# Seven conditional expert tiles, and all loads of the last stage ahead of its outputs

## The chip, the cores and the metric

The kernel runs on one core of one Trainium2 chip. The metric is the time of one execution on the device in microseconds; of several executions the median counts. One further execution was taken by the hardware profiler; its page and trace are what the rows in this document come from. Engines are written as in the profile: PE is TensorE (PEld its weight loads), DVE is VectorE, ACT is ScalarE, POOL is GpSimd, SP is SyncE, which here only issues transfers. A `q` behind a name (SPq, POOLq) is the engine's sequencer.

## The reference

The program computes two layers on an image of 256 channels and 48 x 48 positions, that is 2304 tokens of 256 numbers, all in float32. The first layer is a group norm and a full softmax attention over 9216 rows. The second is a sliced attention and then a mixture of experts. Only the mixture of experts and the way out matter here:

```python
gate_logits = xf @ Wg + bg                      # 2304 tokens x 8 experts
top_w, top_i = jax.lax.top_k(gate_logits, 2)    # two experts for each token
top_w = jax.nn.softmax(top_w, axis=-1)
...
for e in range(E):
    h = jax.nn.gelu(xf @ W1[e] + b1[e], approximate=False)      # 256 -> 1024
    out = out + w_dense[:, e:e + 1] * (h @ W2[e] + b2[e])       # 1024 -> 256
...
t = t + out            # then the tokens are turned back into the image's layout
```

The reference multiplies every token with every expert and weights all but two of the products with zero. So 2 x 2304 = 4608 (token, expert) pairs do count.

## The kernel before

**Tiles of experts.** The kernel sorts the 4608 pairs by expert, and fills tiles of 128 rows, each tile with pairs of one expert only. An expert's last tile is seldom full. How many tiles are needed depends on the data: at least 36 (4608 / 128), and at most 43, which is `NSL = (2 * NT - E) // P + E`. The kernel before always works off 43 tiles. Those that no pair fills belong, by the clamp of `expert_i` to 7, to the last expert, and their rows point at spare rows behind the tokens. Three tables are computed on the chip before the stage begins: `expert_i` (the expert of each tile), `slot_t` (the token's row for each of the 128 rows of each tile) and `slot_w` (the weight of each row). `ends` holds the running sum of the tiles of experts 0 to 7, so its last entry is the number of tiles in use.

**One tile.** `load(s)` gathers 128 normed tokens from DRAM (`tn_d`) into `xs` with an indirect transfer that POOL issues (L1018), and loads the expert's first weights, 1 MB, into `w1` with a transfer that SP issues (L1025). `turn` transposes `xs` on PE into `pt` and DVE copies it to `xT`. `first(s)` multiplies with `w1` into `ph`, and ACT makes `hid` with gelu. `second(s)` multiplies `hid` with `w2_sb`, which holds the second weights of all experts, into `py`; DVE adds the bias and applies the weight into `y`; and POOL issues an indirect transfer that adds `y` to the tokens in DRAM, `t_d` (L1075). Each engine that needs the number of the tile's expert loads it into a register for itself (`expert_of`, L1004).

**The order of the tiles.** The stage is a software pipeline, written out by hand: in round s, `load(s + 2)` is asked for, then `first(s)` is done, then `second(s - 1)`, and after three of the eight steps of that `second` the transposes of tile s + 1 are put in between (`meanwhile`). PE, DVE, ACT and in places POOL keep this written order (the class `InOrder`; each operation issued through it has line L55 in the profile). The indirect transfers and the weight loads are not held to the written order; the framework's scheduler places them. Buffers come from pools: two each of `xs`, `w1`, `xT`, `hid`, `y`, three banks of `ph`, two of `py` and of `pt`.

**The last stage.** The 2304 tokens are read back from `t_d` in five blocks (`TBLOCKS`: four of 512 tokens and one of 256) into `tt`, turned on PE into `pt` (L1127), copied to `ob` by DVE (L1131) and ACT (L1133), and written out (L1134). Loads (L1120) and outputs are both issued by SP, in the order load, output, block by block as the scheduler finds them ready. The pool `fin` has three buffers of `tt` and of `ob`.

**The one condition that is there already.** The attention is computed without subtracting a maximum; the verdict `bad` says whether that was safe. At the end every engine loads `bad` (L1142) and branches (`tc.If(again > 0)`, L1145): the whole program a second time, with the maximum, or nothing. In the runs shown the second pass is not taken. In the arm that is not taken, every engine brings its semaphores to the counts that they would have after the body. L1177 is the program's end, with its drains and the closing barrier.

Of the kernel before, what the change touches and what calls it, by code (L numbers as in the profile page):

```python
# [1 line left out]

# [6 lines left out]
FP = mybir.dt.float32  # L9
AF = mybir.ActivationFunctionType  # L10
ALU = mybir.AluOpType
AX = mybir.AxisListType
PSUM = bass.MemoryType.PSUM

P = 128
C = 256
NT = 2304
# [12 lines left out]
E = 8  # L30
HID = 1024
NHC = HID // P
BIG = 1.5 * 2.0**30


NSL = (2 * NT - E) // P + E


TBLOCKS = [(t, min(512, NT - t)) for t in range(0, NT, 512)]
# [21 lines left out]
def layers(  # L61
# [11 lines left out]
    nc = tc.nc  # L73
    x_v = x[0].rearrange("(c p) h w -> p c (h w)", p=P)
    out_v = out[0].rearrange("(c p) h w -> p c (h w)", p=P)

    const = ctx.enter_context(tc.tile_pool(name="const", bufs=1))
    pe, dve, act, pool = (InOrder(tc, e) for e in (nc.tensor, nc.vector, nc.scalar, nc.gpsimd))
    small = ctx.enter_context(tc.tile_pool(name="small", bufs=2))


# [8 lines left out]
        out=gmat, in_=gmat, pattern=[[-8, 16], [0, 8]], compare_op=ALU.is_ge,  # L90
# [3 lines left out]
        out=gmat, in_=gmat, pattern=[[8, 16], [0, 8]], compare_op=ALU.is_ge,  # L94
# [14 lines left out]
        out=not_before, in_=not_before, pattern=[[-1, P]], compare_op=ALU.is_ge,  # L109
# [96 lines left out]
    for h in range(H1):  # L206
        at = ((h // 2) % 2 * 2 + h // 4) * D1
        nc.sync.dma_start(
            out=Wout_sb[at : at + D1, h % 2, 0:C], in_=Wout[h * D1 : (h + 1) * D1, :]
# [23 lines left out]
    with proj, tc.tile_pool(name="ps_pj", bufs=5, space=PSUM) as ps_pj, tc.tile_pool(  # L233
        name="ps_w", bufs=2, space=PSUM
# [41 lines left out]
        for bi, (t0, tn) in enumerate(TBLOCKS):  # L276
# [6 lines left out]
            for m in range(2):  # L283
# [11 lines left out]
                for j in range(2):  # L295
                    rows = slice(j * DK, (j + 1) * DK)
                    at = (2 * m + j) * NT + t0
# [397 lines left out]
        nc.sync.dma_start(out=w2_sb[:, e], in_=W2[e].rearrange("(f p) d -> p f d", p=P))  # L695
    b2_bc = wts.tile([P, E * C], FP, name="b2_bc")
    nc.sync.dma_start(out=b2_bc, in_=b2.rearrange("e d -> (e d)").partition_broadcast(P))
    fp = ctx.enter_context(tc.tile_pool(name="ffn", bufs=2))
    route = ctx.enter_context(tc.tile_pool(name="route", bufs=1))
    gating = ExitStack()  # L700
    gp = gating.enter_context(tc.tile_pool(name="gate", bufs=1))
# [2 lines left out]
    with tc.tile_pool(name="sa", bufs=1) as sa:  # L704
        tw = sa.tile([P, C + E], FP, name="tw")
        with sums_done, tc.tile_pool(name="ps_b", bufs=4, space=PSUM) as ps_b, tc.tile_pool(
            name="ps_sc", bufs=1, space=PSUM
        ) as ps_sc:
            dve.tensor_tensor(ts_sum, ts_sum, pts, ALU.add)
            ph = ps_b.tile([P, 2, S], FP, name="ph", tag="mm")  # L710
# [63 lines left out]
            a = sa.tile(by_head, FP, name="a")  # L774
# [89 lines left out]
            normed(NTT - 6)  # L864


    expert_i = route.tile([1, NSL], mybir.dt.int32, name="expert_i")
    slot_w = route.tile([P, NSL], FP, name="slot_w")
    slot_t = route.tile([P, NSL], mybir.dt.int32, name="slot_t")
# [2 lines left out]
    with gating, tc.tile_pool(name="onehot", bufs=1) as oh, tc.tile_pool(  # L872
# [121 lines left out]
        ex = gp.tile([P, NSL], FP, name="ex")  # L994
        dve.tensor_reduce(ex, past, AX.X, ALU.add)
        dve.tensor_scalar(expert_i, ex[0:1, :], float(E - 1), None, ALU.min)
        empties = gp.tile([P, NSL], FP, name="empties")
        dve.tensor_scalar(empties, pw[:, 0, :], 0.0, spare, ALU.is_equal, ALU.mult)
        dve.scalar_tensor_tensor(empties, pw[:, 0, :], -1.0, empties, ALU.add, ALU.add)
# [6 lines left out]
            skip_runtime_bounds_check_because="it is counted from 0 and cut at E - 1",  # L1006
        )

    with tc.tile_pool(name="ps_h", bufs=3, space=PSUM) as ps_h, tc.tile_pool(
        name="ps_y", bufs=2, space=PSUM  # L1010
    ) as ps_y, tc.tile_pool(name="ps_t", bufs=2, space=PSUM) as ps_t, tc.tile_pool(
        name="ps_j", bufs=1, space=PSUM
    ) as ps_j:

        def load(s):

            xs = fp.tile([P, C], FP, name="xs", tag="xs")
            nc.gpsimd.indirect_dma_start(  # L1018
                out=xs, out_offset=None, in_=tn_d[:, :],
                in_offset=bass.IndirectOffsetOnAxis(ap=slot_t[:, s : s + 1], axis=0),  # L1020
                bounds_check=NT + P - 1, oob_is_err=True,
            )
            w1 = fp.tile([P, 2, HID], FP, name="w1", tag="w1")
            e = expert_of(s, mybir.EngineType.SP)
            nc.sync.dma_start(  # L1025
                out=w1, in_=W1[bass.ds(e, 1)].rearrange("e (c p) f -> p (e c) f", p=P)
            )
            return xs, w1

        def turn(xs):  # L1030

            pt = ps_t.tile([P, 2, P], FP, name="pt", tag="pt")
            for c in range(2):
                pe.transpose(pt[:, c, :], xs[:, c * P : (c + 1) * P], ident)
            xT = fp.tile([P, 2, P], FP, name="xT", tag="xT")
            dve.tensor_copy(xT, pt)
            return xT

        def first(s, xT, w1):

            e = expert_of(s, mybir.EngineType.Activation)
            hid = fp.tile([P, NHC, P], FP, name="hid", tag="hid")
            for f0 in range(0, NHC, 4):
                ph = ps_h.tile([P, 4, P], FP, name="ph", tag="ph")
                for f in range(f0, f0 + 4):
                    for c in range(2):
                        pe.matmul(
                            ph[:, f - f0, :], w1[:, c, f * P : (f + 1) * P], xT[:, c, :],
                            start=(c == 0), stop=(c == 1),
                        )  # L1050
                for f in range(f0, f0 + 4):
                    act.activation(
                        hid[:, f, :], ph[:, f - f0, :], AF.Gelu, bias=b1_e[:, bass.ds(e, 1), f],
                    )
            return hid

        def second(s, hid, meanwhile):

            e = expert_of(s, mybir.EngineType.PE)
            py = ps_y.tile([P, C], FP, name="py", tag="py")  # L1060
            for f in range(NHC):
                pe.matmul(
                    py, hid[:, f, :],
                    w2_sb[:, bass.ds(e, 1), f, :].rearrange("p e d -> p (e d)"),
                    start=(f == 0), stop=(f == NHC - 1),
                )
                if f == 2:
                    meanwhile()
            e = expert_of(s, mybir.EngineType.DVE)
            y = fp.tile([P, C], FP, name="y", tag="y")  # L1070
            dve.tensor_tensor(
                y, py, b2_e[:, bass.ds(e, 1), :].rearrange("p e d -> p (e d)"), ALU.add
            )
            dve.tensor_scalar(y, y, slot_w[:, s : s + 1], None, ALU.mult)
            nc.gpsimd.indirect_dma_start(  # L1075
                out=t_d[:, :], out_offset=bass.IndirectOffsetOnAxis(ap=slot_t[:, s : s + 1], axis=0),
                in_=y, in_offset=None, bounds_check=NT + P - 1, oob_is_err=True,
                compute_op=ALU.add,
            )

        loaded = {s: load(s) for s in range(2)}
        turned, hid = {}, {}

        def turn_next(s):
            if s < NSL:
                xs, w1 = loaded.pop(s)
                turned[s] = turn(xs), w1

        def judge():

            both = fp.tile([P, 2], FP, name="both", tag="judge")
            for k, op in enumerate((ALU.max, ALU.min)):
                dve.tensor_reduce(both[:, k : k + 1], ends_of[:, k, :], AX.X, op)
            dve.tensor_scalar(both[:, 0:1], both[:, 0:1], HIGH, None, ALU.is_gt)
            dve.tensor_scalar(both[:, 1:2], both[:, 1:2], LOW, None, ALU.is_lt)
            dve.tensor_tensor(both[:, 0:1], both[:, 0:1], both[:, 1:2], ALU.max)
            pm = ps_j.tile([1, P], FP, name="pm")
            pe.transpose(pm, both[:, 0:1], ident)
            dve.tensor_reduce(bad, pm, AX.X, ALU.max)

        turn_next(0)
        for s in range(NSL):
            if s + 2 < NSL:
                loaded[s + 2] = load(s + 2)
            hid[s] = first(s, *turned.pop(s))
            if s == 0:
                turn_next(1)
            else:
                second(s - 1, hid.pop(s - 1), lambda: turn_next(s + 1))
            if s == 4 and bad is not None:  # L1110
                judge()
        second(NSL - 1, hid.pop(NSL - 1), lambda: None)


    with tc.tile_pool(name="fin", bufs=3) as fin, tc.tile_pool(
        name="ps_f", bufs=4, space=PSUM
    ) as ps_f:
        for t0, n in TBLOCKS:
            tt = fin.tile([P, 4, C], FP, name="tt", tag="tt")
            nc.sync.dma_start(  # L1120
                out=tt[:, 0 : n // P, :], in_=t_d[t0 : t0 + n, :].rearrange("(i p) c -> p i c", p=P)
            )
            ob = fin.tile([P, 2, 512], FP, name="ob", tag="ob")
            for c in range(2):
                pt = ps_f.tile([P, 512], FP, name="pt", tag="pt")
                for k in range(n // P):
                    nc.tensor.transpose(  # L1127
                        pt[:, k * P : (k + 1) * P], tt[:, k, c * P : (c + 1) * P], ident
                    )
                if c == 0:  # L1130
                    nc.vector.tensor_copy(ob[:, c, 0:n], pt[:, 0:n])  # L1131
                else:
                    nc.scalar.copy(ob[:, c, 0:n], pt[:, 0:n])  # L1133
            nc.sync.dma_start(out=out_v[:, :, t0 : t0 + n], in_=ob[:, :, 0:n])  # L1134


@with_exitstack
# [44 lines left out]
```

## Time and profile before

| | us |
|---|---|
| median of three executions | 1675.54 (1674.44 to 1675.96) |
| the profiled execution, its own time | 1674.74 |
| its span in the profile | 1672.9 |
| PE busy in the span | 1603.6 (96%) |
| first `xs` gather of the expert stage starts at | 1324.44 |
| last matmul `py` of the expert stage ends at | 1643.23 |
| first load of the last stage starts at | 1649.23 |

Times in rows of the timeline are microseconds from the start of the span: start, duration, engine, line, operation, output and inputs by the program's names, and, in brackets, how long the engine had been idle and what ended that. Rows of the page's slices cut the span into 40 equal parts of 41.8 us; a digit is the busy share in tenths, and PEclk is the clock that TensorE was granted. Durations of matmuls are modelled at their end and overlap a little with the next.

### The profile page before, as it was taken

What the parts mean: (1) busy time and instruction counts of PE and PEld (TensorE: products, weight loads), DVE (VectorE), ACT (ScalarE), POOL (GpSimd) and SP (SyncE); (2) the same over time, 40 slices, a digit from 0 to 9 for tenths busy, and PEclk for the clock granted to TensorE, in tenths of its full rate; (3) what the DMA queues carried; (4) which work ended last, traced back from release to release, by engine and by line L of the source; (5) the groups of instructions that cost most, each with busy time, mean ns of one, the idle gap of its engine ahead of it and who ended that gap; (6) DMA issues with size and microseconds to landing.
All of it is one profiled execution on the core that took longest, in us unless ns stands there. A gap on an engine that the chain in (4) does not pass through costs nothing.

```text
span 1672.9 us, 32258 instructions
## 1 busy us (share of the span) xinstructions
PE 1603.6 (96%) x13376; PEld 821.5 (49%) x13376; DVE 1051.3 (63%) x1371; ACT 819.3 (49%) x1132; POOL 156.5 (9%) x133
## 2 busy tenths in 40 slices
PE   7999999999999999999999999999987699999994
PEld 3633343333333333333333333333334699999994
DVE  6577777778687787787787886877865511111111
ACT  2355565565565555555655655655532133322331
POOL 0000000000000000000000000000001333333331
PEclk9999999999999999999999999999996599999997
DMA  4000000000000000000000000000007366666664
GB/s 132 1 1 1 1 1 1 1 1 1 2 1 1 1 1 2 1 1 1 1 1 1 1 1 1 1 1 1 2 30 269 116 198 174 179 185 189 179 168 125
DMA packets 41267, 82.91 MB, mean 50 GB/s; under 512 B 3693, under 2 KB 26810, under 8 KB 40986
## 3 DMA queue, kind: packets, MB, share of 16 engines
q1 hardware_dynamic: 32858, 69.49, 12.4%
q0 software_dynamic: 8256, 11.28, 3.9%
q8 instruction: 108, 1.77, 0.4%
q14 instruction: 45, 0.37, 0.1%
HBM read 67.78 MB, written 12.98 MB: 48 GB/s over the span
## 4 chain that ended last, share of the span: by engine, by line
PE 77%; issue 11%; POOL 6%; DVE 3%; DMA 2%; ACT 0%; POOLq 0%; SPq 0%; ACTq 0%; DVEq 0%
PE s L55 33%; PE av L55 33%; POOL t_d L1075 3%; POOL xs L1018 2%; PE pa L55 2%; PE ph L55 2%; PE pb L55 1%; DMA t_d<-y,slot_t 1%; PE pw L55 1%; PE py L55 1%; PE pp L288 1%; PE pp L292 1%; PE pp L317 1%; DMA tt<-t_d 0%; DVE s L55 0%
## 5 line engine op out<-in xcount | busy, mean ns | idle before, releaser
L55 DVE TENSOR_TENSOR acc<-acc,p 128x1024 f32<-128x1024 f32 x612 | 748.2, 1223 | 256.6 <-ACT p L55 248.4
L55 ACT ACTIVATE p<-s 128x1024 f32<-128x1024 f32 x648 | 662.7, 1023 | 493.4 <-PE s L55 483.3
L55 PE MATMUL av<-p,v_sb 64*64 64x512 f32 x5184 | 675.8, 590 | 1.4 <-ACT p L55 0.7
L55 PE MATMUL s<-q,kk 64*64 64x512 f32 x5184 | 674.9, 589 | 0.0
L55 PEld LDWEIGHTS s<-q,kk 64*64 64x64 f32 x5184 | 201.9, 133 | 351.3 <-issue 181.0
L55 PEld LDWEIGHTS av<-p,v_sb 64*64 64x64 f32 x5184 | 195.8, 131 | 358.0 <-ACT p L55 201.8
L55 ACT ACTIVATE hid<-ph,bcol 128x128 f32<-128x128 f32 x344 | 98.2, 368 | 238.0 <-PE ph L55 237.9
L55 PEld LDWEIGHTS ph<-xT,w 128*128 128x128 f32 x1376 | 162.6, 194 | 3.0 <-DVE xT L55 0.9
L55 PE MATMUL ph<-xT,w 128*128 128x128 f32 x1376 | 163.0, 278 | 0.5 <-DVE xT L55 0.5
L55 PE MATMUL py<-w_sb,hid 128*128 x688 | 162.1, 379 | 0.0
L55 POOL TENSOR_TENSOR rstd_t<-ve,mhalf 128x1 f32<-128x1 f32 (+1 forms) x21 | 27.5, 1312 | 1251.3 <-DVE ve L55 1251.3
L55 DVE COPY xT<-pt 128x256 f32<-128x256 f32 x43 | 18.3, 425 | 185.4 <-PE pt L55 185.4
L55 PEld LDWEIGHTS py<-w_sb,hid 128*128 128x128 f32 x688 | 124.4, 190 | 13.5
L1075 POOL DMA_INDIRECT t_d<-y,slot_t x43 | 68.2, 1585 | 96.3 <-DVE y L55 91.4
L55 DVE TENSOR_TENSOR y<-py,b_bc 128x256 f32<-128x256 f32 x43 | 18.3, 425 | 80.0 <-PE py L55 80.0
L1018 POOL DMA_INDIRECT xs<-tn_d,slot_t x43 | 45.8, 1064 | 120.5 <-PE pt L55 109.5
L55 DVE RECIPROCAL rinv<-pb 128x256 f32<-128x256 f32 x18 | 31.5, 1751 | 0.0
L55 DVE TENSOR_TENSOR acc<-p 128x1024 f32<-128x1024 f32 x18 | 22.1, 1225 | 8.4 <-ACT p L55 8.4
L305 DVE TENSOR_SCALAR q<-pp,bcol 64x512 f32<-64x512 f32 (+1 forms) x30 | 20.8, 694 | 9.0 <-PE pp L288 8.7
L1127 PE MATMUL pt<-ident,tt 128*128 128x128 f32 x36 | 7.2, 380 | 16.3 <-DMA tt<-t_d 16.3
L55 PE MATMUL pw<-what,t_sb 128*128 128x86 f32 x72 | 15.7, 422 | 6.7 <-POOL what L55 6.7
L55 DVE TENSOR_REDUCE up<-av 128x512 f32<-128x1024 f32 x18 | 21.9, 1217 | 0.0
(247 smaller groups left out, 617.2 us busy)
## 6 DMA issues: line engine op xcount, KB each, us to landing
w<-in_L_ffn_W_dram SPq DMA_DIRECT2D x43, 1024.0 KB, 5.5
w_sb<-in_L_ffn_W_dram SPq DMA_DIRECT2D x8, 1024.0 KB, 10.6
x_sb<-in_x_dram SPq DMA_DIRECT2D x4, 576.0 KB
t_d<-t_sb SPq DMA_DIRECT2D x3, 768.0 KB, 3.9
tn_d<-tn SPq DMA_DIRECT2D x3, 768.0 KB, 3.8
tt<-t_d SPq DMA_DIRECT2D x4, 512.0 KB, 5.1
out_dram<-ob SPq DMA_DIRECT2D x4, 512.0 KB
b_bc<-in_L_ffn_b_dram SPq DMA_DIRECT2D x1, 1024.0 KB
```

Source lines behind the costliest of these rows:

```text
L55: return self.tc.keep_in_program_order(getattr(self.engine, name)(*args, **kwargs))
L288: nc.tensor.matmul(pq[:, 0:tn], WqT[:, c, cols], xn[:, c, toks], start=(c == 0), stop=(c == 1))
L292: nc.tensor.matmul(pk[:, 0:tn], WkT[:, c, cols], xn[:, c, toks], start=(c == 0), stop=(c == 1))
L305: nc.vector.tensor_scalar(dst, pq[rows, 0:tn], bcol[rows, B_Q + m : B_Q + m + 1], 0.125, ALU.add, ALU.mult,)
L317: nc.tensor.matmul(pv[:, 0:C], xn[:, c, i * P : (i + 1) * P], WvT[:, c, :], start=(c == 0), stop=(c == 1),)
L1018: nc.gpsimd.indirect_dma_start(out=xs, out_offset=None, in_=tn_d[:, :], in_offset=bass.IndirectOffsetOnAxis(ap=slot_t[:, s : s + 1], axis= ...
L1075: nc.gpsimd.indirect_dma_start(out=t_d[:, :], out_offset=bass.IndirectOffsetOnAxis(ap=slot_t[:, s : s + 1], axis=0), in_=y, in_offset=None ...
L1127: nc.tensor.transpose(pt[:, k * P : (k + 1) * P], tt[:, k, c * P : (c + 1) * P], ident)
```

## The change

It has two parts.

First, the tiles. The first 36 (`SURE`) are worked off in the software pipeline as before; `load(s + 2)` is now written after `first(s)`, and stops with tile 36. Then the number of tiles in use, `used_i`, is loaded by every engine, and tiles 36 to 42 follow, each inside a condition that lies inside the one before: tile s is done if `used > s`. In each block the load of tile s + 1, `first(s)` and `second(s)` of the same tile follow each other; the transposes of tile s + 1 are still put inside `second(s)`. When a condition fails, all that is nested in it is skipped. Buffers are no longer taken from pools tile by tile: the same number of buffers is made once, and a cycle walks through them (`ring`).

Second, the last stage. SP is held to the written order for its transfers too, the five loads are written ahead of everything else, and the pool has five buffers of `tt` and of `ob`.

```diff
+SURE = 2 * NT // P
...
+        dve.tensor_scalar(used_i, ends[0:1, E - 1 : E], float(NSL), None, ALU.min)
...
+        def ring(pool, n, shape, name):
+            return cycle([pool.tile(shape, FP, name=f"{name}{k}") for k in range(n)])
+
+        ring_xs, ring_w1 = ring(fp, 2, [P, C], "xs"), ring(fp, 2, [P, 2, HID], "w1")
+        ring_xT, ring_hid = ring(fp, 2, [P, 2, P], "xT"), ring(fp, 2, [P, NHC, P], "hid")
+        ring_y = ring(fp, 2, [P, C], "y")
+        ring_ph, ring_py = ring(ps_h, 3, [P, 4, P], "ph"), ring(ps_y, 2, [P, C], "py")
+        ring_pt = ring(ps_t, 2, [P, 2, P], "pt")
...
-        for s in range(NSL):
-            if s + 2 < NSL:
+        for s in range(SURE):
+            hid[s] = first(s, *turned.pop(s))
+            if s + 2 <= SURE:
                 loaded[s + 2] = load(s + 2)
-            hid[s] = first(s, *turned.pop(s))
             if s == 0:
                 turn_next(1)
             else:
                 second(s - 1, hid.pop(s - 1), lambda: turn_next(s + 1))
             if s == 4 and bad is not None:
                 judge()
-        second(NSL - 1, hid.pop(NSL - 1), lambda: None)
-
-
-    with tc.tile_pool(name="fin", bufs=3) as fin, tc.tile_pool(
+        second(SURE - 1, hid.pop(SURE - 1), lambda: None)
+        used = nc.values_load(
+            used_i, min_val=0, max_val=NSL,
+            skip_runtime_bounds_check_because="it is a sum of counts, cut at NSL",
+        )
+        with ExitStack() as more:
+            for s in range(SURE, NSL):
+                more.enter_context(tc.If(used > s))
+                if s + 1 < NSL:
+                    loaded[s + 1] = load(s + 1)
+                second(s, first(s, *turned.pop(s)), lambda: turn_next(s + 1))
+
+
+    with tc.tile_pool(name="fin", bufs=len(TBLOCKS)) as fin, tc.tile_pool(
         name="ps_f", bufs=4, space=PSUM
     ) as ps_f:
+        tts = []
         for t0, n in TBLOCKS:
             tt = fin.tile([P, 4, C], FP, name="tt", tag="tt")
-            nc.sync.dma_start(
+            tts.append(tt)
+            sp.dma_start(
                 out=tt[:, 0 : n // P, :], in_=t_d[t0 : t0 + n, :].rearrange("(i p) c -> p i c", p=P)
             )
+        for (t0, n), tt in zip(TBLOCKS, tts):
             ob = fin.tile([P, 2, 512], FP, name="ob", tag="ob")
...
-            nc.sync.dma_start(out=out_v[:, :, t0 : t0 + n], in_=ob[:, :, 0:n])
+            sp.dma_start(out=out_v[:, :, t0 : t0 + n], in_=ob[:, :, 0:n])
```

`expert_i`, `slot_t` and `slot_w` are still computed for 43 tiles.

## The prediction

> **What bounds the kernel now.** I read the 40 slices of the page first, then the timeline of the expert stage and of the end, then the instructions of the existing condition (L1145) one engine at a time.
>
> ```profile
> PE   7999999999999999999999999999987699999994
> PEclk9999999999999999999999999999996599999997
> ```
>
> The expert stage is slices 32 to 39: TensorE is full there and its clock is whole. Nearly all of the rest of the span belongs to the attention, which the diff does not touch. One expert tile looks like this:
>
> ```profile
> 1581.85 3.73 PE L55 MATMUL ph<-xT,w 128*128 128x128 f32 x32
> 1582.05 0.42 DVE L55 TENSOR_TENSOR y<-py,b_bc 128x256 f32<-128x256 f32 x1 [1.74 <-PE py L55]
> 1583.15 1.59 POOL L1075 DMA_INDIRECT t_d<-y,slot_t  x1 [1.96 <-DVE y L55]
> ...
> 1586.72 0.38 PE L55 MATMUL pt<-ident,xs 128*128 128x128 f32 x2
> 1586.94 2.32 PE L55 MATMUL py<-w_sb,hid 128*128 x10
> 1587.38 1.06 POOL L1018 DMA_INDIRECT xs<-tn_d,slot_t  x1 [2.64 <-PE pt L55]
> ```
>
> The next `ph` starts at 1589.10, so a tile is 7.25 us, bound by TensorE. The gather of a later tile (L1018) is issued right after a transpose, four microseconds ahead of the scatter, and has a whole tile to land. The end of the stage:
>
> ```profile
> 1636.16 7.07 PE L55 MATMUL py<-w_sb,hid 128*128 x32
> ...
> 1645.35 1.55 POOL L1075 DMA_INDIRECT t_d<-y,slot_t  x1 [2.89 <-DMA t_d<-y,slot_t]
> 1649.23 6.57 SPq L1120 DMA_DIRECT2D tt<-t_d  x4
> ...
> 1662.25 0.43 SPq L1120 DMA_DIRECT2D tt<-t_d  x1
> ...
> 1667.27 0.37 SPq L1134 DMA_DIRECT2D out_dram<-ob  x1
> ```
>
> Every scatter waits for the one before it to land. The last matmul ends at 1643.23, the last scatter lands at 1649.14 (chain of waits: 3.79 us), the first load of the last stage follows, and the fifth load is issued only at 1662.25, behind four outputs in SP's queue. From 1649.23 to the end is 23.7 us. What a condition costs is shown by the one at the end (each row: engine's sequencer, count, ns, when):
>
> ```profile
> L1145 PEldq EVENT_SEMAPHORE  x2: 51/51/51, 1669.6 to 1669.7; - x2
> L1145 POOLq COMPARE_BRANCH  x1: 53/53/53, 1645.7 to 1645.7; - x1
> L1145 POOLq INC_SWDGE_SEM  x1: 1184/1184/1184, 1649.4 to 1649.4; - x1
> L1145 PEldq COMPARE_BRANCH  x1: 3395/3395/3395, 1666.1 to 1666.1; - x1
> ```
>
> Each engine loads the number and branches alone: POOL does so 21 us before PE. There is no barrier at the entry. In the arm not taken each engine waits for its own work and adds to its semaphores what the skipped body would have; POOL also waits for its DMAs and runs INC_SWDGE_SEM. The jump over the long body took PE 3.4 us; POOL's first instruction after it came 2.6 us later.
>
> [...] the granted clock changes on multiples of 3.41 us (1647.88, 1658.12, 1661.53), and around 1250 us a window with PE busy 51% was followed by half clock, one with 58% was not. [...] in the trace gathers land 2.8 to 5.5 us after issue, but none follows a scatter directly.
>
> **How many tiles go.** The trace can't show it; the data do. The reference's routing of its own inputs sends 638, 617, 565, 585, 503, 586, 536 and 578 tokens to the eight experts. In tiles of 128: 5, 5, 5, 5, 4, 5, 5, 5, that is 39. So tiles 36 to 38 run under conditions and 39 to 42 are skipped.
>
> **Step 1, the four skipped tiles:** 4 x 7.25 = 29.0 us of PE off the path.
>
> **Step 2, the three conditional tiles lose the overlap.** A block is not mixed with what is outside it. In block s POOL first has the scatter of tile s-1 in front of it, and only then can it issue the gather of tile s+1. Count from T, the end of the previous `py`. The scatter starts at T+1.30 (1583.15 after 1581.85) and takes 1.59; with a gap of 0.2 to 0.3 the gather starts at T+3.1. PE needs it for the transpose at T+4.87 (1586.72). The gather lands after 2.8 (least seen, T+5.9) to 5.4 us (T+8.5). I take 3.6, the highest of the first three gathers of the stage, which ran without a weight load beside them (3.2, 2.8, 3.6): here it stands behind the scatter instead, while `w1` of the next tile, whose 5.5 us load delays gathers today, is mostly out of the way, since SP reaches it early. So PE waits T+6.7 - T+4.87 = 1.85 us in each block (1.1 to 3.6). The first block has 0.9 more: `py` of tiles 34 and 35 run back to back, and the scatter of 35 waits for that of 34, as the last two do now. Sum: 3 x 1.85 + 0.9 = 6.45 us. Dropping the software pipeline itself costs PE nothing: `hid` of the first half is ready 0.5 us before `ph` ends, and the second half (gelu 0.29 us each) is ahead of the 0.45 us per `py` step. Tile 39's load and transpose are still done in block 38; they are in the three waits.
>
> **Step 3, clock.** A wait of 1.85 us inside one 3.41 us window is 54% of it idle, at the threshold. Where it drops, one window at half clock loses some 1.7 us of work. I take two thirds of that per block: 3 x 1.1 = 3.3 us (0 to 5).
>
> **Step 4, branches.** Three taken entries fall through, some 0.05 to 0.1 us on sequencers that run ahead (PE's branch at 1666.1 came before its last matmul was done). The number's own loads (0.3 to 0.5 us an engine, once) lie beside step 2's waits. The jump over tiles 39 to 42 costs at most 3.4 us per engine: PE's is covered by the 10 us it waits for the first load, SP's by the scatter, POOL's by the scatter's landing, which is how it goes now (1645.71 to 1648.35). Not covered: INC_SWDGE_SEM, after the last scatter has landed and before SP may load `t_d`. Now it ends 1.48 us after the landing; so 1.5 us. Against it, the last scatter no longer queues behind another: T+1.30 instead of 1645.35 - 1643.23 = 2.1, a gain of 0.8. Net +0.6 (with 0.1 for the joins). The joins' short jumps: 0 to 1 us.
>
> **Step 5, the last stage.** All five loads are issued within about 2.4 us and no output stands before the fifth. Three loads (1.5 MB) land 7.0 us after the first issue (1656.21); reads run at about 0.37 MB/us, so 0.75 MB more is 9.1. PE, then still at half clock, finishes blocks at about +6, 8, 9.3 as now, then 10.4 and 10.9; the last output is issued at +11.6 instead of +18.0. Outputs (0.4 MB/us, 2.25 MB) follow the reads on the same queue and land near +15.0. From the last issue to the end is now 5.6 us (SP's load of `bad`, its far jump, the semaphores): +17.2 instead of +23.7, a gain of 6.5 (4 to 7.5). DMA becomes the bound here; that is why not more.
>
> **Sum**, against the profiled execution (1674.74 us, span 1672.9): -29.0 + 6.45 + 3.3 + 0.6 - 6.5 = -25.1, so 1649.6. That execution lies 0.8 us under the median of 1675.54, so a median of about 1650.
>
> **Rivals.**
> - *Everything is covered:* the gather lands in 2.8 us and the clock holds. Steps 2 and 3 fall to 4.2, and with a last stage at its best the gain is 32: 1643. For it: two of those three gathers took 3.2 us or less. Against: none followed a scatter.
> - *Each block pays in full:* landing 5.4 us, half clock every time, and PE's entries stall too. 3 x 3.6 + 0.9 + 5 = 16.7, last stage 4: gain 15.7, 1659. A far jump at each of the seven entries and joins, 3.4 us each and all on the path, would take the whole gain (no change); the trace has it only where thousands of instructions are jumped, and most engines would hide it.
> - *Slower: too few tiles are skipped.* A conditional tile costs 3.25 us more than a plain one (9.75 / 3), so with k skipped the gain is 7.25k - 3.25(7 - k) + 5.9. At k = 2 it is 4.2, at k = 1 it is -6.3: 1681. It decides from 42 used tiles on. Expert 0 is two tokens short of a full fifth tile, which could make 40 (k = 3, 1660), but 42 needs counts that the reference does not give.
> - *It does nothing:* used_i reads as 43 and all arms run: k = 0, some 17 us slower. `ends` is the running sum of tiles per expert, its last entry the total, so I see no reason.
>
> **How the numbers follow.** Main case 0.75; everything covered 0.08; full price 0.11; no change 0.02; slower 0.04. A difference under 0.2% (3.4 us) can't be told from none. The range takes in the gather's landing, the clock and the last stage: 1642 to 1661.
>
> **What would show it.** Four `w1` loads and four pairs of indirect DMAs fewer (39 scatters, 40 gathers); three PE waits of about 2 us before `pt<-ident,xs` from 1597 us on, ended by the gather, each gather starting right after a scatter; INC_SWDGE_SEM between the last scatter's landing and the first `tt` load near 1631; five `tt` loads in a row and a stage of 17 us. It is wrong if blocks begin with all engines waiting, if PE stalls at entries, or if other than 39 scatters run.

## The result and the profile after

The changed kernel takes 1650.49 us (median of four, 1649.36 to 1651.68) against 1674.99 us (median of four, one execution more than in the table above); the ratio is 0.9855, with a 95% interval of 0.9838 to 0.9872. Its profiled execution took 1650.91 us with a span of 1649.2; the one before had 1674.74 and 1672.9. The forecast was a median of about 1650, so the sum came out within half a microsecond. Its terms did not: the two that were furthest off were wrong by 1.5 and 1.6 us in opposite directions. That the sum is so close is therefore luck in part, as the part on the prediction works out.

The slices of the page after, PE and its granted clock (tenths, 40 slices of 41.2 us):

```profile
PE   7999999999999999999999999999997589999984
PEclk9999999999999999999999999999996689999998
```

They look as before: the attention is untouched and PE is full almost to the end. The gain and what eats at it lie in the last 57 us. This is the timeline of the three conditional tiles and of the last stage (start, duration, engine, line, operation; in brackets the idle time ahead and what ended it):

```profile
1592.57 3.73 PE L57 MATMUL ph<-xT,w 128*128 128x128 f32 x32
1594.89 1.55 POOL L1090 DMA_INDIRECT t_d<-y,slot_t  x1 [2.94 <-PE ph L57]
1596.14 1.46 PE L57 MATMUL py<-w_sb,hid 128*128 x6
1596.75 1.10 POOL L1033 DMA_INDIRECT xs<-tn_d,slot_t  x1 [0.30 <-issue]
1601.87 0.69 PE L57 MATMUL pt<-ident,xs 128*128 128x128 f32 x2 [4.27 <-DMA xs<-tn_d,slot_t]
1602.35 4.47 PE L57 MATMUL py<-w_sb,hid 128*128 x10
1606.62 3.91 PE L57 MATMUL ph<-xT,w 128*128 128x128 f32 x32
...
1609.84 1.10 POOL L1033 DMA_INDIRECT xs<-tn_d,slot_t  x1 [0.30 <-issue]
1614.21 0.44 PE L57 MATMUL pt<-ident,xs 128*128 128x128 f32 x2 [2.39 <-DMA xs<-tn_d,slot_t]
...
1619.83 1.10 POOL L1033 DMA_INDIRECT xs<-tn_d,slot_t  x1 [0.30 <-issue]
1622.66 0.44 PE L57 MATMUL pt<-ident,xs 128*128 128x128 f32 x2 [0.98 <-DMA xs<-tn_d,slot_t]
1622.93 2.32 PE L57 MATMUL py<-w_sb,hid 128*128 x10
...
1626.39 1.58 POOL L1090 DMA_INDIRECT t_d<-y,slot_t  x1 [5.46 <-DVEq L1132]
1630.38 2.95 SPq L57 DMA_DIRECT2D tt<-t_d  x5
...
1637.26 4.77 SPq L57 DMA_DIRECT2D out_dram<-ob  x5
```

Three things are to be seen. Each block has one idle of PE, always ahead of `pt<-ident,xs` and always ended by the gather: 4.27, 2.39 and 0.98 us. Each gather (L1033) starts 0.30 us after POOL has ended its own part of a scatter (L1090, 1.55 to 1.58 us in these rows; the bytes land 3.8 to 3.9 us after the row's start). And after the first wait the same ten `py` matmuls take 4.47 us instead of 2.32: PE is at half clock (0.50 in the windows below). The five loads of the last stage leave within 3 us, and all five outputs follow.

The clock is plain where the stretch is cut at steps of 3.41 us, on which the granted clock changes in this trace (length, busy us of PE, PEld, DVE, ACT and POOL with their instructions, then PEclk, DMA share, GB/s):

```profile
1596.73:1600.14 3.41, 0.87 (x5) 0.42 (x3) 0.00 (x0) 0.82 (x4) 1.10 (x1) 1.00 0.97 265
1600.14:1603.55 3.41, 1.68 (x5) 1.50 (x6) 0.42 (x1) 0.00 (x0) 0.00 (x0) 0.50 0.29 119
1603.55:1606.97 3.42, 3.42 (x10) 2.72 (x9) 0.11 (x1) 0.00 (x0) 0.00 (x0) 0.50 0.02 5
1606.97:1610.38 3.41, 3.41 (x33) 3.41 (x32) 0.67 (x2) 1.14 (x4) 2.12 (x2) 1.00 0.11 7
1610.38:1613.79 3.41, 1.44 (x8) 0.94 (x6) 0.00 (x0) 1.14 (x4) 0.56 (x1) 1.00 0.74 208
```

The window with PE busy 0.87 of 3.41 us is followed by two at 0.50; the one with 1.44 is not followed by a fall (the next has 1.00). The first also shows what the DMA engines do while PE waits: they are 97% busy.

The conditions themselves, from the instructions of the line that holds them (engine's sequencer, count, ns least/median/most, first and last start):

```profile
L1132 PEldq COMPARE_BRANCH  x5: 65/93/3326, 1589.1 to 1627.1; - x5
...
L1132 POOLq COMPARE_BRANCH  x5: 34/37/53, 1595.3 to 1628.7; - x5
...
L1132 POOLq INC_SWDGE_SEM  x1: 1775/1775/1775, 1626.9 to 1626.9; - x1
```

The entries that fall through cost 34 to 93 ns. One jump, PE's over the four skipped tiles, took 3.3 us, beside a wait of 9.3 us for the first load. INC_SWDGE_SEM, which POOL runs in the arm not taken, ran from 1626.9 to 1628.7, while the last scatter was still on its way. The chain of waits has nothing between that scatter and the first load but 0.16 us of SP's own:

```profile
1626.39 3.84 DMA t_d<-y,slot_t
...
1630.38 4.04 DMA tt<-t_d
```

### The profile page after: what moved, and what is told of

The parts are those of the page before. It is cut to its first block, busy times and chain, and to the rows that moved or that the text cites. A ratio compares the mean times of both kernels' runs of the same rounds, so it can differ in the third digit from the quotient of the medians.

```text
span 1649.2 us, 31729 instructions
## 1 busy us (share of the span) xinstructions
PE 1576.2 (96%) x13178; PEld 795.1 (48%) x13178; DVE 1046.9 (63%) x1361; ACT 810.0 (49%) x1100; POOL 147.1 (9%) x126
## 4 chain that ended last, share of the span: by engine, by line
PE 92%; DVE 3%; DMA 2%; issue 2%; ACT 0%; POOL 0%; SPq 0%; ACTq 0%; POOLq 0%; DVEq 0%
PE s L57 33%; PE av L57 33%; PE ph L57 8%; PE py L57 8%; PE pa L57 2%; PE pb L57 1%; PE pw L57 1%; PE pp L292 1%; PE pp L296 1%; PE pp L321 1%; DMA t_d<-y,slot_t 1%; PE pt L57 1%; DMA Wq_raw<-in_L_conv_Wq_dram 0%; DVE s L57 0%; PE pm L57 0%
## 5 line engine op out<-in xcount | busy, mean ns | idle before, releaser
L57 ACT ACTIVATE hid<-ph,bcol 128x128 f32<-128x128 f32 x312 | 89.0, 368 | 231.2 <-PE ph L57 217.6
L57 PEld LDWEIGHTS ph<-xT,w 128*128 128x128 f32 x1248 | 148.0, 195 | 3.0 <-DVE xT L57 0.9
L57 PE MATMUL py<-w_sb,hid 128*128 x624 | 149.3, 383 | 0.0
L57 PE MATMUL ph<-xT,w 128*128 128x128 f32 x1248 | 148.3, 278 | 0.5 <-DVE xT L57 0.5
L57 PEld LDWEIGHTS py<-w_sb,hid 128*128 128x128 f32 x624 | 114.2, 193 | 12.7
L1090 POOL DMA_INDIRECT t_d<-y,slot_t x39 | 61.8, 1585 | 101.5 <-DVE y L57 91.2
L1033 POOL DMA_INDIRECT xs<-tn_d,slot_t x40 | 42.6, 1066 | 105.7 <-PE pt L57 96.2
L57 PE MATMUL pt<-ident,xs 128*128 128x128 f32 x80 | 16.2, 283 | 11.8 <-DMA xs<-tn_d,slot_t 11.8
```

Of the source, the lines that this page charges most:

```text
L57: return self.tc.keep_in_program_order(getattr(self.engine, name)(*args, **kwargs))
L1033: nc.gpsimd.indirect_dma_start(out=xs, out_offset=None, in_=tn_d[:, :], in_offset=bass.IndirectOffsetOnAxis(ap=slot_t[:, s : s + 1], axis= ...
L1090: nc.gpsimd.indirect_dma_start(out=t_d[:, :], out_offset=bass.IndirectOffsetOnAxis(ap=slot_t[:, s : s + 1], axis=0), in_=y, in_offset=None ...
```

## The experiments

Changes of a few microseconds are read inside the stage, since the stage itself begins up to 2.4 us earlier or later from one profiled execution to another (the first conditional `ph` between 1590.4 and 1592.8). "Ratio" is against the kernel before.

**The two parts alone.** In the first kernel the last stage is as it was:

```diff
-    with tc.tile_pool(name="fin", bufs=len(TBLOCKS)) as fin, ...
+    with tc.tile_pool(name="fin", bufs=3) as fin, ...
...                     # nc.sync instead of sp, each load written in its block's turn
```

> The conditional tiles alone, with the last stage as it was (three buffers, loads and outputs in the old order). Theory: the two parts are independent, one ends where the first load of tt starts. In the trace of the changed kernel that load starts at 1630.4 instead of 1649.2 us, so this kernel should gain 18.9 us: 1656 us, 39 scatters, and a last stage of 23.7 us. Rival: the earlier end of the expert stage brings the last stage into leftover traffic or another clock, and the parts do not add: then the gain differs from 18.9 by more than 2 us.

Measured: 1655.77 us, ratio 0.9892 (0.9875 to 0.9908). The first load is at 1629.96 and the span ends at 1654.1, a last stage of 24.1 us:

```profile
1629.96 6.40 SPq L1145 DMA_DIRECT2D tt<-t_d  x4
```

In the second, the tiles are as before and only the last stage is new:

```diff
+        for t0, n in TBLOCKS:
+            ...
+            sp.dma_start(out=tt[:, 0 : n // P, :], in_=...)
+        for (t0, n), tt in zip(TBLOCKS, tts):
...
-        for t0, n in TBLOCKS:
```

> The last stage alone (five loads first, five buffers), with all 43 tiles unconditional as before. The sum on record had 6.5 us for it; the trace of the changed kernel shows a stage of 18.8 us instead of 23.7, that is 4.9. Theory: 4.9 us less, 1670 us, with the outputs' DMA and SP's slow far jump at the end. Rival: the stage was only slowed by what the conditional tiles left behind, and alone it gains the full 6.5 us: 1668.5.

Measured: 1669.47 us, ratio 0.9970 (0.9958 to 0.9983). The span ends at 1667.9, so the stage takes 18.6 us, 5.1 less than before and not the rival's 6.5:

```profile
1649.26 2.63 SPq L55 DMA_DIRECT2D tt<-t_d  x5
```

The ratios multiply to 0.9862, within the interval of the whole change: the parts are independent, they meet at the first load. The conditional tiles bring about 18 us, the last stage 4 to 5 (the medians differ by 17.6 and 3.9).

**What do the conditions cost?** Two kernels: one without conditions, with the number of tiles written in,

```diff
-        for s in range(SURE):
+        for s in range(39):
...
-                more.enter_context(tc.If(used > s))
```

> The changed kernel with 39 tiles all in the software pipeline and no condition around them (the number is fixed for this data). It prices the conditions: theory, they cost only three PE waits for gathers (4.3 + 2.4 + 1.0 us) and one stretch of half clock (2.6 us), less 0.7 us for the last scatter that here queues behind another: 9.6 us less than the changed kernel, 1641 us. Rival: entries, joins and the jump cost on the path too: then this kernel is faster by more than 11 us.

and one with all conditions kept, in which the gather is asked for two tiles ahead (three `xs` buffers; the weights one tile ahead as before; the gather of tile 37 moves into the last round of the pipeline):

```diff
             for s in range(SURE, NSL):
                 more.enter_context(tc.If(used > s))
+                if s + 2 < NSL:
+                    rows[s + 2] = gather(s + 2)
                 if s + 1 < NSL:
-                    loaded[s + 1] = load(s + 1)
+                    loaded[s + 1] = weights(s + 1)
```

> The changed kernel with three xs buffers and the gather asked for two tiles ahead in the conditional blocks too; everything else, conditions included, is kept. Theory: the three PE waits end because the gather is no longer needed in the block that issues it, and with them the half clock: 10.2 us less than the changed kernel, 1640.3 us, no idle of PE before pt<-ident,xs after tile 35. Rival: the wait is taken over by the weight load or by the branches: PE still waits in each block, and the gain is under 5 us.

Measured: 1639.28 us without conditions, ratio 0.9796 (0.9780 to 0.9813), and 1640.25 us with the gather ahead, ratio 0.9800 (0.9783 to 0.9816). Beside the changed kernel's 0.9855 the differences are 9.9 and 9.2 us. (The medians themselves differ by 11.2 and 10.2, but the kernel before was 1.6 us faster beside these two than beside the changed kernel. Inside the stage, from the `ph` of tile 35 to the first load, it is 10.2 and 10.8: 48.51 us in the changed kernel, 38.29 without conditions, 37.75 with the gather ahead.) The timeline of the gather-ahead kernel, first conditional block and part of the second:

```profile
1596.74 1.10 POOL L1033 DMA_INDIRECT xs<-tn_d,slot_t  x1 [0.31 <-issue]
...
1597.47 0.38 PE L57 MATMUL pt<-ident,xs 128*128 128x128 f32 x2
1597.69 2.32 PE L57 MATMUL py<-w_sb,hid 128*128 x10
...
1604.72 0.38 PE L57 MATMUL pt<-ident,xs 128*128 128x128 f32 x2
```

A gather starts where it did, but it is that of the tile after, and PE does not wait for it: no brackets at `pt`, `py` at 2.32 us, blocks 7.25 us apart. From the first conditional `ph` to the first load are 27.05 us, against 37.81 in the changed kernel. So both theories hold, and the rivals fall: entries, joins and jumps do not show on the path, since the conditions without the waits are as fast as no conditions, within 1 us. This kernel beats both of the pair.

**All seven tiles run.** `used_i` is forced to 43, in the changed kernel and in the one with the gather ahead:

```diff
-        dve.tensor_scalar(used_i, ends[0:1, E - 1 : E], float(NSL), None, ALU.min)
+        dve.tensor_scalar(used_i, ends[0:1, E - 1 : E], float(NSL), None, ALU.max)
```

> The changed kernel with used_i forced to 43, so that all seven conditional tiles run. By the record's formula (a conditional tile costs 7.25 + 3.25 us, the rest gains 5.9) it should be 16.9 us slower than the kernel before: 1692. With the waits seen in the trace: blocks whose gather meets a weight load wait 2.4 to 4.3 us, and half clock follows in some, so four more blocks of 9.6 to 12 us: 38 to 48 us more than the changed kernel, 1689 to 1698. Rival: the waits die out from block to block as in the trace (4.3, 2.4, 1.0): four more blocks of 8 us, 1683.

> The gather two tiles ahead (as in e4) with used_i forced to 43, so that seven conditional tiles run and none is skipped. Theory: with the gather out of the way a conditional tile costs what a plain one does, 7.25 us: four tiles more than e4 are 29 us, less 0.7 us nowhere given back, 1669 us, below the kernel before. Rival: a condition has a price of its own on PE's path that the three blocks of e4 were too few to show, half a microsecond or more a block: 1671 or above.

Measured (one execution each): 1692.27 us and 1668.12 us, beside 1674.17 and 1673.82 for the kernel before. PE's timeline of the first, from the third wait on:

```profile
1623.74 0.69 PE L57 MATMUL pt<-ident,xs 128*128 128x128 f32 x2 [3.39 <-DMA xs<-tn_d,slot_t]
...
1634.97 0.44 PE L57 MATMUL pt<-ident,xs 128*128 128x128 f32 x2 [1.00 <-DMA xs<-tn_d,slot_t]
...
1646.22 0.49 PE L57 MATMUL pt<-ident,xs 128*128 128x128 f32 x2 [3.78 <-DMA xs<-tn_d,slot_t]
...
1656.37 0.44 PE L57 MATMUL pt<-ident,xs 128*128 128x128 f32 x2 [1.00 <-DMA xs<-tn_d,slot_t]
```

The waits do not die out. From the first conditional `ph` to the first load it is 79.68 us, that is 41.87 for four more tiles, 10.5 each. The recorded price of 3.25 us over a plain tile, and with it 1692, is met: with no tile to skip the change would be a loss of 18 us. With the gather ahead it is 55.65 us, so four more tiles cost 28.6 us, 7.15 each, and even with nothing skipped that kernel stays 5.7 us below the kernel before, about what the last stage brings.

**Why is the gather late?** The weight loads are left out of the conditional blocks (tiles 37 and 38 are multiplied with older weights):

```diff
-                    loaded[s + 1] = load(s + 1)
+                    loaded[s + 1] = load(s + 1, weights=False)
```

> The changed kernel without the weight loads in the conditional blocks (tiles 37 and 38 are multiplied with older weights). Theory: the gathers landed after 5.1, 4.3 and 2.8 us because a 1 MB weight load ran beside the first two and none beside the third. Without it all three land in about 2.8 to 3.2 us; PE waits 2.0 to 2.4, 1.0 and 1.0 us, and the clock does not fall: 4.5 to 6 us less than the changed kernel. Rival: the gather is late because it stands behind the scatter in the software queue: the landings stay at 4 to 5 us.

Measured: 1645.52 us in one execution, 28.65 less than the kernel before beside it. Time from issue to landing of the three gathers, in the changed kernel and then without the weight loads (least, median, most):

```profile
DMA to landing us min/median/max: 2.8/4.3/5.1
```

```profile
DMA to landing us min/median/max: 2.8/2.9/2.9
```

All three stand behind a scatter in both kernels; only the weight load is gone. In the changed kernel SP issues these two:

```profile
1596.34 0.37 SPq L1040 DMA_DIRECT2D w<-in_L_ffn_W_dram  x1
```

```profile
1610.56 0.37 SPq L1040 DMA_DIRECT2D w<-in_L_ffn_W_dram  x1
```

0.4 us before the first gather (landing 5.07 us) and 0.7 after the second (4.33); the third gather has none beside it (2.79). These are not the weights of the tile that is gathered, which came a block earlier (tile 37's at 1585.63), but those of the tile after: SP runs a block ahead. PE's waits without them are 2.03, 1.07 and 1.05 us. From `ph` to the first load it is 33.45 us, 4.4 less, just short of the 4.5 expected. The theory holds for the landings, and the rival of the queue falls; but the clock fell after the 2.03 us wait against my expectation:

```profile
1595.08:1598.49 3.41, 1.38 (x8) 0.92 (x7) 0.00 (x0) 0.94 (x4) 1.10 (x1) 1.00 0.47 77
1598.49:1601.90 3.41, 3.41 (x10) 2.69 (x9) 0.42 (x1) 0.00 (x0) 0.00 (x0) 0.50 0.00 0
```

Here a window with 1.38 us busy was followed by half clock, in the changed kernel one with 1.44 was not. In the other runs with such waits the conditional blocks divide at the same place: of the windows at whole clock, those with 1.19 us or less were followed by half clock, those with 1.46 or more were not.

**Why was INC_SWDGE_SEM off the path?** Tile 38 is skipped too:

```diff
-        dve.tensor_scalar(used_i, ends[0:1, E - 1 : E], float(NSL), None, ALU.min)
+        dve.tensor_scalar(used_i, ends[0:1, E - 1 : E], 38.0, None, ALU.min)
```

> The changed kernel with used_i cut at 38: tile 38 is left out, so the output lacks its rows. The step on record that put INC_SWDGE_SEM between the last scatter's landing and the first load (1.5 us) failed: it ran 1.5 us before that landing. Theory: POOL's arm waits only for those of the eight software queue semaphores that the skipped body would have raised, and with seven skipped transfers the last scatter's is the eighth. With 38 tiles nine transfers are skipped, all eight are raised, so INC_SWDGE_SEM must follow the landing: first tt load 1.8 to 2.0 us after the landing instead of 0.16. Rival: the arm never waits for the last scatter: 0.2 us again.

Measured: 1644.25 us in one execution. The instructions of the condition, and the first load:

```profile
L1132 POOLq EVENT_SEMAPHORE  x4: 17/43/43, 1620.8 to 1621.1; - x4
...
L1132 POOLq INC_SWDGE_SEM  x1: 1724/1724/1724, 1621.2 to 1621.2; - x1
```

```profile
1623.11 2.85 SPq L57 DMA_DIRECT2D tt<-t_d  x5
```

The last scatter is issued at 1616.87 and lands 3.94 us later, at 1620.81:

```profile
DMA to landing us min/median/max: 3.9/3.9/3.9
```

POOL's waits end behind it, INC_SWDGE_SEM follows, and SP starts its load 2.3 us after the landing instead of 0.16, somewhat more than the 1.8 to 2.0 expected; the instruction took 1.72 us, where at the end of the kernel before it took 1.18. The theory holds, and the semaphores that the instructions of the two traces name say the same. In the changed kernel POOL's arm waits for 112 to 117 and 119, the last scatter raises 118, and only SP waits for that one. With 38 tiles POOL waits for all of 112 to 119; the last scatter's is 116, and it is the first that POOL waits for. So of these two kernels the one with nine software transfers in the skipped body has the arm not taken on the path, and the one with seven has not.

**Buffers or order in the last stage?** Five buffers, but SP's transfers written and issued as before:

```diff
-            sp.dma_start(out=out_v[:, :, t0 : t0 + n], in_=ob[:, :, 0:n])
+            nc.sync.dma_start(out=out_v[:, :, t0 : t0 + n], in_=ob[:, :, 0:n])
```

> The changed kernel with five buffers in the last stage but with its loads and outputs written and issued as before (SP not held to the written order). It tells the buffers from the order. The program that results issues four loads, four outputs, and only then the fifth load. Theory: the order is what counts. The fifth load leaves at about +11 instead of +2 us after the first, lands 3 to 4 us later, and the last output follows at +16: a stage of 21.5 to 23 us against 18.8, so 1653.5 to 1655. Rival: the DMA engines' bytes set the end whatever the order: 19 us.

Measured: 1652.24 us in one execution, with a stage of 23.2 us from the first load to the end. SP's queue:

```profile
1627.35 2.02 SPq L1145 DMA_DIRECT2D tt<-t_d  x4
...
1634.07 4.16 SPq L1159 DMA_DIRECT2D out_dram<-ob  x4
...
1638.58 0.37 SPq L1145 DMA_DIRECT2D tt<-t_d  x1
...
1644.67 0.38 SPq L1159 DMA_DIRECT2D out_dram<-ob  x1
```

The total is below the expected 1653.5 because in this execution the first load comes at 1627.35 instead of 1630.38; the stage itself is 0.2 above its range. The fifth load leaves 11.2 us after the first, as expected. The order is what counts: five buffers alone gain 0.5 us of the 23.7.

**What sets the end?** The condition at the very end, with the second pass, is left out:

```diff
-    again = tc.nc.values_load(bad, ...)
-    with tc.If(again > 0):
-        layers(tc, None, *args)
```

> The changed kernel without the condition at its end (the second pass over the whole program, which was not taken, is left out). It asks what sets the end of the last stage, 7.6 us after the last output's issue instead of 5.6: SP's load of bad (1.15 us) and its far jump (3.6 us) among the outputs' traffic, or the outputs' landing (16.3 us after the first load). Theory: both end within 0.3 us of each other, so without the jump the end follows the landing: span shorter by 0.5 to 1.5 us. Rival: the jump alone is late, and 3 us go.

Measured: 1647.72 us in one execution. The span ends at 1645.9:

```profile
1628.86 3.08 SPq L57 DMA_DIRECT2D tt<-t_d  x5
```

The stage is 17.1 us instead of 18.8, so 1.7 went, 0.2 more than expected: the last output lands 0.5 us earlier, 15.75 instead of 16.26 us after the first load, and the other 1.2 lay between that landing and the end. The 0.5 may be no effect of the jump: in the other runs with the new order that landing comes at 16.0 to 17.1. The size is nearer to the theory's 0.5 to 1.5 than to the rival's 3: most of the slow jump lies beside the outputs' landing. In the changed kernel the sequencers' loads of `bad` and their far jump ran among the outputs:

```profile
L1170 SPq TENSOR_LOAD <-bad x1: 1150/1150/1150, 1642.1 to 1642.1; - x1
```

```profile
L1173 SPq EVENT_SEMAPHORE  x9: 17/17/17, 1646.9 to 1647.5; - x9
...
L1173 PEldq COMPARE_BRANCH  x1: 4167/4167/4167, 1641.1 to 1641.1; - x1
...
L1173 SPq COMPARE_BRANCH  x1: 55/55/55, 1643.3 to 1643.3; - x1
```

SP branches at 1643.3 and its next instruction comes at 1646.9: 3.6 us, where the kernel before had 2.6; the load of `bad` took 1.15 us instead of 0.28:

```profile
L1142 SPq TENSOR_LOAD <-bad x1: 276/276/276, 1667.7 to 1667.7; - x1
```

The other runs tell whether the conditional tiles or the outputs' traffic make this slow. With the old order of the last stage, where SP branches behind the last, lone output, SP's load and jump take 0.28 and 2.61 us (conditional tiles alone) and 0.29 and 2.78 (five buffers). With the new order they take 0.84 to 1.16 and 3.3 to 3.9, the last stage alone (0.86 and 3.28) and the kernel without conditions (0.84 and 3.78) included. So it goes with the order and not with the tiles.

## Why the prediction was right, point by point

**Step 1, four tiles skipped, -29.0: right.** The page after has 39 scatters, 40 gathers and 40 weight loads. The count of 39 from the reference's routing held.

**Step 2, waits, +6.45: right in place and in what PE waits for, 7.6 measured** (4.27 + 2.39 + 0.98). The recorded T+3.1 for the gather's start is met (3.2 in the second and third block; 4.2 in the first, where the scatter of tile 35 came late as predicted). The term that was mis-sized is the landing, 3.6 us in each block: it was 5.07, 4.33 and 2.79. The reason given with it was wrong: the weights of the next tile were out of the way, but those of the tile after it were not. That load waits for the `first` of the block to free its buffer. In the first two blocks `first` ends at 1596.30 and 1610.53, the load starts at 1596.34 and 1610.56, the gather at 1596.75 and 1609.84, and the two run together. Without weight loads the landing is 2.8 to 2.9 us, which is also the least seen in the kernel before: standing behind the scatter added nothing that these landings show. One reading of the kernel before was off without a part in the sum: the gather at 1587.38 is 3.0 us ahead of the next scatter (1590.40), not four.

**Step 3, clock, +3.3: right in kind, 2.9 measured.** From `ph` to `ph` the first block takes 14.05 us: 7.25, the wait of 4.27, and 2.5 of half clock. The second has another 0.4. It was one fall of two windows, not two thirds of a window in each block. The recorded threshold, near half of a window, was the author's estimate from two windows of the kernel before (51% busy and then half clock, 58% busy and then whole clock). It does not hold for these matmuls: the second block's window was busy for 1.44 of 3.41 us, 42%, and kept the clock.

**Step 4, branches, net +0.6: wrong, -0.9 measured.** From PE's last `py` at 1625.25 to the first load it is 5.1 us, before it was 6.0. Entries, joins and jumps were hidden, as argued. (The record's own terms, 1.5 - 0.8 + 0.1, make +0.8, not +0.6.) The failed step is "Not covered: INC_SWDGE_SEM, after the last scatter has landed", 1.5 us: I read it off the condition at the end of the program, whose arm waits for all eight semaphores of the software queue, on which POOL's indirect transfers go (112 to 119 in that trace). This arm skips seven such transfers and waits for seven semaphores; the last scatter's is the eighth, and SP waits for that one itself. The run with 38 tiles, where nine are skipped, brings the wait back (2.3 us from the landing to the first load).

**Step 5, last stage, -6.5: right in kind, -4.9 measured.** The last output leaves at +11.2 (recorded +11.6), so loads, transposes and copies went as worked out. What failed is "From the last issue to the end is now 5.6 us": it took 7.6. That tail had been measured where the last output ran alone. Moved in among the other outputs, the last one lands later than worked out (+16.3 instead of +15.0), and SP's load of `bad` and its far jump, which run beside that landing, take 1.9 us more.

**The sum** is -29.0 + 7.6 + 2.9 - 0.9 - 4.9 = -24.3; the spans differ by 23.7. The remaining 0.6 is not the stage's start: the `first` of tile 36 begins at 1592.57, behind 3.5 us of the `second` of tile 35, and in the kernel before at 1589.10 ahead of them. Most of it lies in the third block. From its `ph` (1616.65) to the end of its `py` (1625.25) it takes 8.60 us, 1.2 more than the same block with the gather ahead, and the wait explains 0.98 of these; and both hold the transposes of tile 39, which nothing uses, some 0.22 us that the last tile of the kernel before does not have. The recorded -25.1 was close because step 4 erred by +1.5 and steps 2 and 5 the other way, by 1.2 and 1.6. That they cancel is luck.

**Rivals.** "Slower: too few tiles are skipped" was not the case here, but its formula was tried, and with it "It does nothing": 17 us slower worked out for none skipped, 18 measured. "Each block pays in full" came true in the first block alone (landing 5.07 us and half clock). "Everything is covered" is what the gather-ahead kernel makes true, though not by the fast landing that the rival supposed: its three gathers land 4.9, 5.5 and 2.8 us after issue, but none is needed in the block that issues it.

## What to carry to other kernels

The conditions here have no barrier at their entry (in the changed kernel SP branches at the first one at 1579.1 us, POOL at 1595.3). Their price here, about 9 us, was a gather that was no longer asked for early; the kernel with the gather ahead does not pay it. So look at every transfer that the unconditioned loop issued ahead, and ask for it a block earlier, with one more buffer if need be. When a load is moved, find out which other load its new time falls beside; here 1 MB of weights made a gather of 128 KB land 1.5 to 2.3 us later. And a tail measured where the last output ran alone can be longer once the change has put it among others, here 7.6 us instead of 5.6.

## What was not expected of the hardware

- In two kernels the arm not taken waited for the queue semaphores that the skipped body would have raised: for seven of the eight with seven skipped software transfers, for all eight with nine. The first load came 0.16 us after the last scatter's landing with seven, 2.3 us with nine.
- Sequencers were slower among the outputs' transfers: loading one number took 1.15 us on SP and 0.78 to 0.92 on PE, DVE and ACT where the kernel before had about 0.3, and SP's far jump 3.6 us instead of 2.6. Over all runs it goes with the order of the last stage; why the load of one number takes longer there is not shown.
- PE's busy time in a window of 3.41 us, as the profile shows it, did not tell by itself whether half clock followed. Among the expert tiles' matmuls 1.44 us of 3.41 kept the clock whole and 1.38 did not. In the kernel before, other matmuls lost it with more: 1.49 us with the transposes of the last stage (the window from 1658.12 to 1661.53), and 1.72 us, half of the window, behind the attention:

```profile
1251.93:1255.35 3.42, 1.72 (x12) 1.44 (x12) 2.10 (x11) 1.63 (x6) 0.00 (x0) 1.00 1.00 348
```

What decides it is not shown.
